# A GNN, attention and expert layer: the edge count, the turned tiles, the keys' copies, the stores and the norm's groups rearranged

## The chip, the core and the metric

The kernel runs on one core of one Trainium2 chip. It is written against the core's engines: TensorE (PE in the profile; the loads of its weights are listed apart as PEld), VectorE (DVE), ScalarE (ACT), GpSimd (POOL) and SyncE (SP), which only issues transfers. ScalarE and GpSimd also issue transfers from their own instruction streams; the profile lists these issues as ACTq, POOLq or POOL DMA_DIRECT2D. The metric is the time of one execution in microseconds (us), lower is better. All data are float32, apart from the 0/1 masks of the edge count, which are bfloat16.

## What is computed

N = 1250 rows of D = 768 features, and E = 21,250 edges (10,000 random pairs in both directions, and a loop at each node) sorted by their target. Cut to what matters:

```python
edge_index = jnp.stack([src, dst])
xn = _layernorm(x)
x = x + gnn(xn, edge_index) + mix(xn)
x = x + ffn(_layernorm(x))

def gnn(x, edge_index):          # two graph attention layers, then one product
    x_norm = layer_norm(x, norm_g, norm_b)
    out1 = gat_conv(x_norm, ..., W1, 4 heads of 192)
    out2 = gat_conv(out1, ..., W2, 2 heads of 96)
    return concatenate([x, out2]) @ Wu + bu

def mix(x):                      # linear attention, 12 heads of 64, then an MLP
    h = layer_norm(x, ln1_w, ln1_b)
    q, k, v = split(h @ qkv_w + qkv_b); q, k = elu(q) + 1, elu(k) + 1
    kv = einsum('hsd,hse->hde', k, v); z = 1 / einsum('hsd,hd->hs', q, k.sum(s))
    x = x + einsum('hde,hsd,hs->hse', kv, q, z) @ proj_w + proj_b
    h = layer_norm(x, ln2_w, ln2_b)
    return x + gelu(h @ fc1_w + fc1_b) @ fc2_w + fc2_b

def ffn(x):                      # 4 experts, the gates from the mean over all rows
    ...
```

gat_conv weighs each edge by a softmax over the edges of its target. The same pair can occur several times among the edges, and then counts as often.

## The kernel before

**Tiles and stages.** The rows are cut into NT = 10 tiles of TP = 125; the 768 features into KC = 6 parts of 128 for TensorE's contraction, and into two output halves of 384 (HALVES). Two large buffers, slot_a and slot_x, hold changing things: acc (L67) is ten tiles of raw x in slot_a, xn (L68) ten normalized tiles in slot_x, and fT [128, 6, 1250] the rows turned (features on partitions). The stages, in time order (us from the span's start):

1. to 32: the attention vectors are folded into W1 (turned_weights, folded); the result is fx.
2. 31 to 120: the loop over tiles at L488: normalized(t) (L404, one ScalarE instruction) writes xn; six transposes ps_t (L496) and two ScalarE copies (L499) turn the tile into fT; ps_u (L503) is the tile times Wu, 24 TensorE instructions, and VectorE adds it to acc (L508). So each tile's products begin with transposes and end before the next tile's transposes.
3. 120 to 213, the "g loop" at L527: norms(t + 1) (L467) brings the next tile through two more norms: a transpose of the row scales (ps_r, L472), a VectorE product into zT or in place into fT (L480), and six affines for each, alternating between VectorE (even k, L338) and ScalarE (odd k, L334). Then ps_g (L536) is zT times fx, 24 instructions; ScalarE copies it into gt (L541), VectorE copies the attention scores s (L542), and SyncE stores gt to g1_d in DRAM. zT and gt have two buffers each in the pool pk.
4. 213 to 297 keys, then values, queries (375 to 460), products of quarters: each pair of tiles needs seven products (a Strassen form) with the intermediate tiles c1, u2 and ex (keys_pair L614, values_pair L654, queries L698).
5. 457 to 541: the projection ps_p (L913), with a norm after it in groups of tiles, order2 (L900): moments on VectorE, then z on ScalarE (L936), six transposes (L943) and affines into fT.
6. 541 to 1357: the MLP (fc1 L127 and L81, fc2 L1016) mixed with the two graph attention layers; 1357 to the end: the experts.

**Edges.** The attention is computed on a dense matrix of edge counts, tabs[0] and tabs[1] in DRAM. Each edge has a key (target times N plus source, kcol: one column of 125 keys for each of 170 groups). edge_piece(i) (L282) handles 17 columns: kr (L275, 1 MB, the keys of these groups broadcast to all partitions) is compared with kcol (L292, eq), summed (L296, mult: how often the edge's key occurs in its group), multiplied by a lower triangle mask `before` (L297), summed again (L301, first), turned into first = 0 or 1 (L302), and then into a place (L304, L307): the key itself for the first occurrence, a row of trash otherwise. 17 indirect scatters from POOL (L309) add mult at place, alternately to the two tables. Pieces 0 to 5 are placed in the ps_u loop at tiles 1, 2, 4, 5, 7, 8 (`pieces`), pieces 6 to 9 in the g loop at odd tiles. The keys of pieces 0 to 3 are loaded from POOL's queue, each issued where piece i − 2 is (load_keys, L272); the later ones from SyncE's. The scatters to one table wait for each other's landing.

**What sets the order.** The program is written in one stream; the framework places the waits from the reads and writes of tiles and from the reuse of buffers, and may move instructions of one engine ahead of each other by its own priorities, except where the helpers `pin`, `vec`, `act`, `mat` (L71 to L83) keep the written order. So the built order is not the written one: among others, the first (k = 0) matmuls of some tiles' ps_g stand before the rest of an earlier tile's.

**Stores.** by_parts (L91) splits each store of a tile in two issues (112 and 13 partitions) and pins it. In the g loop raw x goes to raw_d (at t = 4 and 5, five tiles each, from ScalarE's queue) and xn to xn_d (at t = 6 to 9, two, two, two and four tiles, from ScalarE's queue too). Both are read back later: xn_d before the projection, raw_d in the graph stage. slot_x is then overwritten by the keys: y1 and y2 in keys_pair are kk, a view of slot_x.

**Places.** Keys' and values' c1, u2 and kex are tiles of the pool kvp, opened after pk is closed and so laid into the place of zT and gt; queries' copies qc1, qu2, qex lie in the pool qp, together with z2 (L934, one buffer) of the norm stage. The pool mk (opened at t == 8 in the g loop on the right side, where the edges' pool ep was before edges.close()) holds wsum, same, kvbd, ksum and later wq.

Of the kernel before, what the change touches and what calls it, by code (L numbers as in the profile page):

```python
# [8 lines left out]
F32 = mybir.dt.float32  # L9
# [17 lines left out]
PIECE = 17  # L27
# [5 lines left out]
def tile_gps_layer(ctx, tc, a, out):  # L33
# [212 lines left out]
    def columns():  # L246
# [12 lines left out]

    before = ep.tile([128, TP], BF16, name="before")  # L260
    nc.gpsimd.memset(before, 1.0)
    nc.gpsimd.affine_select(
        out=before, in_=before, compare_op=ALU.is_ge, fill=0.0, base=-1,
# [18 lines left out]
    def edge_piece(i):  # L282
# [13 lines left out]
        nc.vector.tensor_reduce(mult[:, c0 : c0 + PIECE], eq, AX.X, ALU.add)  # L296
        nc.vector.tensor_tensor(  # L297
            eq, eq, before[:TP].unsqueeze(1).to_broadcast([TP, PIECE, TP]), ALU.mult
        )
        first = ep.tile([TP, PIECE], F32, name="first", bufs=2)  # L300
        nc.vector.tensor_reduce(first, eq, AX.X, ALU.add)  # L301
        nc.vector.tensor_scalar(first, first, 0.0, None, op0=ALU.is_equal)  # L302
# [185 lines left out]
    for t in range(NT):  # L488
        tc_ = slice(t * TP, (t + 1) * TP)
        if t:  # L490
            normalized(t)
        for j in range(2):
            ps = bank4("ps_t")
            for i in range(3):
                k = 3 * j + i
                nc.tensor.transpose(  # L496
                    ps[:, i, :TP], xn[:, t, k * 128 : (k + 1) * 128], ident[:TP, :TP]
                )
            nc.scalar.copy(fT[:, 3 * j : 3 * j + 3, tc_], ps[:, :3, :TP])  # L499
        for c0, w in HALVES:  # L500
            ps = bank("ps_u")
            for k in range(KC):
                nc.tensor.matmul(  # L503
                    ps[:TP, :w], fT[:, k, tc_], wu[:, k, c0 : c0 + w],
                    start=k == 0, stop=k == KC - 1,
                )
            o = acc[:, t, c0 : c0 + w]
            nc.vector.tensor_tensor(o, ps[:TP, :w], o, ALU.add)  # L508
        for t0, n in SPLITS[1:]:
            if t == t0 - 2:  # L510
                for t1 in range(t0, t0 + n):
                    moments(acc[:, t1, :], mv[:, t1, :], vec)
                scales(t0, n)
        if t == 8:
            ahead = norms(0)
        if t in pieces:
            edge_piece(pieces[t])
# [9 lines left out]
    for t in range(NT):  # L527
# [21 lines left out]
        if t in (4, 5):  # L549
            for i in range(5 * t - 20, 5 * t - 15):  # L550
                by_parts(nc.scalar, raw_d[i], acc[:, i, :])
        if t > 5:
            for i in ((0, 5), (1, 6), (2, 7), (3, 8, 4, 9))[t - 6]:
                by_parts(nc.scalar, xn_d[i], xn[:, i, :])
# [16 lines left out]
        if t == 8:  # L571
            edges.close()
            mk = mix.enter_context(tc.tile_pool(name="mk", bufs=1, side="right"))
            wsum = mk.tile([128, 3, 3, 384], F32, name="wsum")
            wk7 = seven_weights(wk, wsum)
            by_tokens(nc.vector, xt, 0, TP)
# [9 lines left out]
    with tc.tile_pool(name="kvp", bufs=1) as kvp:  # L586
# [27 lines left out]
        def keys_pair(t):  # L614
# [4 lines left out]
            c1 = u3 = kvp.tile([TP, 384], F32, name="c1", bufs=2)  # L619
            u2 = kvp.tile([TP, 384], F32, name="u2", bufs=2)  # L620
# [3 lines left out]
            def put(o, p, q):  # L624

                nc.vector.tensor_tensor(o, p, q, ALU.add)
                ex = kvp.tile([TP, 384], F32, name="kex", bufs=2)
# [26 lines left out]
        def values_pair(t, vs):  # L654
# [4 lines left out]
            c1 = u3 = kvp.tile([TP, 384], F32, name="c1", bufs=2)  # L659
            u2 = kvp.tile([TP, 384], F32, name="u2", bufs=2)  # L660
# [37 lines left out]
        def queries(i, c):  # L698
# [5 lines left out]
            c1 = u3 = qp.tile([128, 375], F32, name="qc1", bufs=2)[:, :w]  # L704
            u2 = qp.tile([128, 375], F32, name="qu2", bufs=2)[:, :w]
# [4 lines left out]
            def put(o, p, k):  # L710
                ex = qp.tile([128, 375], F32, name="qex", bufs=2)[:, :w]
# [122 lines left out]
    with tc.tile_pool(name="qp", bufs=1) as qp:  # L834
# [65 lines left out]
        order2 = [(0, 1, 5, 6), (2, 3, 7), (4, 8, 9)]  # L900
# [4 lines left out]
        for part in order2:  # L905
# [27 lines left out]
            for t in part:  # L933
                z = qp.tile([TP, D], F32, name="z2", bufs=1)  # L934
# [865 lines left out]
```

## Time and profile before

| what | us |
|---|---|
| runs | 1912.76, 1917.06, 1915.63 (median 1915.63) |
| the profiled execution, its own time | 1917.79 |
| its span on the core | 1915.70 |
| TensorE's granted clock, mean over the span | 0.993 |
| busy: ScalarE / GpSimd | 802.8 / 502.7 |

The span is from the first to the last instruction that the profiler saw; the profiled execution's own time is 2.09 us longer. Busy times of the engines by stage, from the table of stretches (PE, VectorE and ScalarE, and PE's granted clock in it):

| stretch | length | PE | DVE | ACT | clock |
|---|---|---|---|---|---|
| 31 to 120, ps_u | 89.0 | 86.07 | 64.42 | 18.46 | 1.00 |
| 112 to 226, g loop to keys' start | 114.0 | 102.69 | 96.36 | 33.95 | 0.96 |
| 226 to 243, first keys | 17.0 | 15.86 | 9.50 | 6.07 | 0.85 |
| 243 to 541, keys to projection | 298.0 | 297.46 | 165.42 | 74.42 | 1.00 |
| 541 to 556, the last norm group | 15.0 | 10.71 | 9.12 | 8.92 | 0.89 |

Lines of the timeline begin with the start and the duration of an instruction, or of several alike joined together (x6), both in us; then engine, line, operation, output and inputs; and in brackets how long the engine had been idle before, and what ended it. Lines of the groups give busy time and the mean in ns of one instruction after the first bar, and the idle time just before them after the second.

### The profile page before, as it was taken

Reading aid. Unit: us, or ns where it says so; the run is one execution under the profiler, and the core shown is the slowest. Engines: PE = TensorE matmul, PEld = TensorE weight load, DVE = VectorE, ACT = ScalarE, POOL = GpSimd, SP = SyncE. Lnnn points to the kernel's source line nnn. Section 1 sums busy time; section 2 is a strip of 40 time slices with the busy share of each in tenths; the row PEclk is TensorE's granted clock in tenths of the full one; section 3 lists DMA queues with packets and bytes.
Section 4 is the critical chain, followed back from the end, with each engine's and each line's share of the span. In section 5 each row is a group of like instructions: output and inputs, shape, how many; then the busy total and the mean of one; then the engine's idle time right before and its main releaser. Section 6 shows DMA issues by size and latency. Waiting matters only on the chain.

```text
span 1915.7 us, 19523 instructions
## 1 busy us (share of the span) xinstructions
PE 1872.7 (98%) x6966; PEld 1244.2 (65%) x6966; DVE 1355.5 (71%) x2372; ACT 802.8 (42%) x1206; POOL 502.7 (26%) x341
## 2 busy tenths in 40 slices
PE   8999899999999999999999999999999999999998
PEld 7555456775556667787877655566766666666664
DVE  4889651379545986676766977865787777777778
ACT  3223231232321117777775166754473343533330
POOL 2167588777851110020210111100131000000000
PEclk9999999999999999999999999999999999999999
DMA  9957711423149742242432542301485201011023
GB/s 342 274 133 177 200 1 2 116 18 66 2 34 158 142 111 76 70 118 74 113 100 56 149 121 82 92 9 52 130 95 90 76 1 66 1 66 38 20 85 110
DMA packets 184284, 175.49 MB, mean 92 GB/s; under 512 B 110043, under 2 KB 153595, under 8 KB 182908
## 3 DMA queue, kind: packets, MB, share of 16 engines
q0 software_dynamic: 126640, 68.01, 20.7%
q1 hardware_dynamic: 54270, 98.48, 16.3%
q10 hardware_dynamic: 3278, 7.75, 1.3%
q8 instruction: 55, 0.90, 0.2%
q14 instruction: 41, 0.34, 0.1%
HBM read 137.80 MB, written 42.05 MB: 94 GB/s over the span
## 4 chain that ended last, share of the span: by engine, by line
PE 87%; DMA 5%; DVE 3%; issue 2%; ACT 1%; SPq 1%; POOL 0%; DVEq 0%; POOLq 0%; ACTq 0%
PE ps_f L1016 15%; PE ps_p L81 13%; PE ps_r L81 12%; PE ps_a L127 8%; PE ps_o L1194 7%; PE ps_p L913 4%; PE ps_c L127 4%; PE ps_g L536 3%; PE ps_f L1594 3%; PE ps_o L1233 2%; PE ps_va L127 2%; PE ps_qa L127 2%; PE ps_ka L127 2%; PE ps_d L127 2%; PE ps_u L1246 1%
## 5 line engine op out<-in xcount | busy, mean ns | idle before, releaser
L309 POOL DMA_INDIRECT tab<-mult,place_e x170 | 355.7, 2092 | 149.5 <-DMA tab<-mult,place_e 99.0
L1016 PE MATMUL ps_f<-w,v 128*125 128x384 f32 x960 | 337.5, 486 | 0.0
L1016 PEld LDWEIGHTS ps_f<-w,v 128*125 128x125 f32 x960 | 177.7, 188 | 106.0 <-issue 7.5
L1021 DVE TENSOR_TENSOR slot_a<-ps_f,slot_a 125x384 f32<-125x384 f32 x240 | 131.5, 552 | 66.5 <-PE ps_f L1016 62.6
L1149 DVE TENSOR_TENSOR wt<-ee 125x375 f32<-125x375 f32 (+1 forms) x180 | 105.8, 589 | 85.8 <-PE ps_o L1194 57.5
L1194 PEld LDWEIGHTS ps_o<-turns,wt 125*125 125x125 f32 x800 | 136.9, 188 | 29.7 <-DVE wt L1150 4.5
L1194 PE MATMUL ps_o<-turns,wt 125*125 125x193 f32 x800 | 151.6, 329 | 3.5 <-DVE wt L1150 3.5
L1144 ACT ACTIVATE ee<-bt,s 125x375 f32<-125x375 f32 (+1 forms) x180 | 114.8, 638 | 78.0 <-DVE wt L1149 69.5
L81 PE MATMUL ps_p<-fT,w 128*128 128x312 f32 (+1 forms) x432 | 125.5, 426 | 2.1 <-DMA w<-in_L_ffn_w_dram 1.5
L1150 DVE SCALAR_TENSOR_TENSOR wt<-wt,slot_x 125x375 f32<-125x375 f32 (+1 forms) x180 | 105.9, 589 | 4.4
L81 PEld LDWEIGHTS ps_p<-fT,w 128*128 128x128 f32 x432 | 81.5, 189 | 37.9 <-issue 1.7
L81 PE MATMUL ps_r<-w,slot_a 128*125 128x384 f32 x260 | 94.5, 486 | 0.0
L536 PE MATMUL ps_g<-fx,zT 128*125 128x388 f32 x240 | 83.6, 507 | 5.7 <-DVE zT L338 5.2
L127 PE MATMUL ps_a<-fT,w 128*128 128x250 f32 (+1 forms) x288 | 85.4, 426 | 0.7 <-DVE slot_a L918 0.7
L1556 DVE SCALAR_TENSOR_TENSOR slot_x<-ps_r,gate,slot_x 125x384 f32<-125x384 f32 x100 | 60.7, 615 | 33.3 <-PE ps_r L81 33.0
L81 PE MATMUL ps_p<-xt,ws 128*128 128x313 f32 (+1 forms) x288 | 83.6, 425 | 0.0
L503 PE MATMUL ps_u<-wu,fT 128*125 128x384 f32 x240 | 80.0, 490 | 2.4 <-ACT fT L499 2.4
L913 PE MATMUL ps_p<-wp,slot_x 128*125 128x384 f32 x240 | 79.5, 486 | 0.0
L1086 DVE SCALAR_TENSOR_TENSOR slot_x<-turns,s,slot_x 125x1250 f32<-125x1250 f32 x54 | 79.4, 1509 | 0.1
L1147 ACT ACTIVATE ee<-bt,s1l 125x375 f32<-125x375 f32 (+1 forms) x120 | 75.4, 628 | 0.1
L965 ACT ACTIVATE v<-v,par 128x250 f32<-128x250 f32 (+1 forms) x72 | 40.0, 556 | 78.1 <-DVE v L985 31.7
L81 PE MATMUL ps_r<-w2s,ht 128*125 128x384 f32 x200 | 72.7, 486 | 0.0
(403 smaller groups left out, 3432.1 us busy)
## 6 DMA issues: line engine op xcount, KB each, us to landing
turns<-g_d POOLq DMA_DIRECT2D x12, 942.4 KB
w<-in_L_mix_fc_w_dram SPq DMA_DIRECT2D x12, 768.0 KB
w<-in_L_mix_fc_w_dram SPq DMA_DIRECT2D x24, 384.0 KB
slot_x<-tab POOLq DMA_DIRECT2D x14, 610.4 KB
w<-in_L_ffn_w_dram SPq DMA_DIRECT2D x11, 768.0 KB
w<-in_L_ffn_w_dram SPq DMA_DIRECT2D x5, 1536.0 KB
slot_x<-tab POOLq DMA_DIRECT2D x40, 183.1 KB
kr<-key_d SPq DMA_DIRECT2D x6, 1062.5 KB
```

The lines of the kernel that those rows point to most:

```text
L81: return lambda *args, **kw: pin(getattr(self.engine, name)(*args, **kw))
L127: engine.matmul(ps, wt[:, k, :], x[:, k, :], start=k == 0 and not more, stop=k == n - 1, skip_group_check=more,)
L309: nc.gpsimd.indirect_dma_start(out=tabs[c % 2][:, :], out_offset=bass.IndirectOffsetOnAxis(ap=place[:, c : c + 1], axis=0), in_=mult[:, c ...
L503: nc.tensor.matmul(ps[:TP, :w], fT[:, k, tc_], wu[:, k, c0 : c0 + w], start=k == 0, stop=k == KC - 1,)
L536: nc.tensor.matmul(ps[:TP, :388], zT[:, k, :], fx[:, k, h2 * 388 : (h2 + 1) * 388], start=k == 0, stop=k == KC - 1,)
L913: nc.tensor.matmul(ps[:TP, :w], qT[:, k, t * TP : (t + 1) * TP], pm[:, k, c0 : c0 + w], start=k == 0, stop=k == KC - 1,)
L1016: nc.tensor.matmul(ps, v_of[c][:, f, h, at : at + TP], lasts[g, j][:, f, :], start=f == 0, stop=f == 1,)
L1021: nc.vector.tensor_tensor(o, ps, o, ALU.add)
L1144: nc.scalar.activation(e[:, 0, :w], bt[:TP, 0, :w], AF.Exp, bias=s[:, 0, h, c : c + 1])
L1149: nc.vector.tensor_tensor(wt[:, :w], e[:, 0, :w], e[:, 1, :w], ALU.max)
L1150: nc.vector.scalar_tensor_tensor(wt[:, :w], wt[:, :w], 1.0, adj, op0=ALU.min, op1=ALU.mult)
L1194: nc.tensor.matmul(sums[i // 2][:TP, (i % 2) * 193 : (i % 2 + 1) * 193], wt[:, i * TP : (i + 1) * TP], gh[:, c, :], start=c == 0 and i % 2 ...
```

## The change

It has five parts.

1. `before` holds 256 on and 1 off the strict lower triangle, in place of 1 and 0. One reduction after the multiplication gives mult, and first is mult < 256. The reduction of eq before the multiplication falls away. For an edge that is the first of its key in its group the sum is the old count; for another it is larger, and such edges go to the trash rows.
2. The transposes and copies of a tile become a function, turned_x; turned_x(t + 1) stands between the two halves of tile t's ps_u, and normalized(t + 1) before them.
3. c1, u2 and ex of keys, values and queries come from one helper, between, with two buffers each of [128, 384] in the pool mk.
4. raw_d is stored at t = 2 and 3 of the g loop (five tiles each), xn_d at t = 4 to 8 (two tiles each).
5. The last group (4, 8, 9) of the norm becomes (4, 8) and (9,), and z2 has two buffers.

```diff
--- before.py
+++ after.py
@@ -257,10 +257,11 @@
     before = ep.tile([128, TP], BF16, name="before")
-    nc.gpsimd.memset(before, 1.0)
+    nc.gpsimd.memset(before, 256.0)
     nc.gpsimd.affine_select(
-        out=before, in_=before, compare_op=ALU.is_ge, fill=0.0, base=-1,
+        out=before, in_=before, compare_op=ALU.is_ge, fill=1.0, base=-1,
         pattern=[[-1, TP]], channel_multiplier=1,
     )
     mult = const.tile([TP, EC], F32, name="mult")
@@ -293,13 +294,12 @@
             eq, kr[:TP], kcol[:, c0 : c0 + PIECE].unsqueeze(2).to_broadcast([TP, PIECE, TP]),
             ALU.is_equal,
         ))
-        nc.vector.tensor_reduce(mult[:, c0 : c0 + PIECE], eq, AX.X, ALU.add)
         nc.vector.tensor_tensor(
             eq, eq, before[:TP].unsqueeze(1).to_broadcast([TP, PIECE, TP]), ALU.mult
         )
+        nc.vector.tensor_reduce(mult[:, c0 : c0 + PIECE], eq, AX.X, ALU.add)
         first = ep.tile([TP, PIECE], F32, name="first", bufs=2)
-        nc.vector.tensor_reduce(first, eq, AX.X, ALU.add)
-        nc.vector.tensor_scalar(first, first, 0.0, None, op0=ALU.is_equal)
+        nc.vector.tensor_scalar(first, mult[:, c0 : c0 + PIECE], 256.0, None, op0=ALU.is_lt)
         at = ep.tile([TP, PIECE], F32, name="at_e", bufs=2)
         nc.vector.scalar_tensor_tensor(
             at, kcol[:, c0 : c0 + PIECE], trash, first, op0=ALU.subtract, op1=ALU.mult
@@ -485,10 +485,8 @@
         return zT
 
     pieces = {1: 0, 2: 1, 4: 2, 5: 3, 7: 4, 8: 5}
-    for t in range(NT):
-        tc_ = slice(t * TP, (t + 1) * TP)
-        if t:
-            normalized(t)
+
+    def turned_x(t):
         for j in range(2):
             ps = bank4("ps_t")
             for i in range(3):
@@ -496,8 +494,18 @@
                 nc.tensor.transpose(
                     ps[:, i, :TP], xn[:, t, k * 128 : (k + 1) * 128], ident[:TP, :TP]
                 )
-            nc.scalar.copy(fT[:, 3 * j : 3 * j + 3, tc_], ps[:, :3, :TP])
+            nc.scalar.copy(
+                fT[:, 3 * j : 3 * j + 3, t * TP : (t + 1) * TP], ps[:, :3, :TP]
+            )
+
+    turned_x(0)
+    for t in range(NT):
+        tc_ = slice(t * TP, (t + 1) * TP)
+        if t + 1 < NT:
+            normalized(t + 1)
         for c0, w in HALVES:
+            if c0 and t + 1 < NT:
+                turned_x(t + 1)
             ps = bank("ps_u")
             for k in range(KC):
                 nc.tensor.matmul(
@@ -546,11 +554,11 @@
         by_parts(nc.sync, g1_d[:, t * TP : (t + 1) * TP, :].rearrange("h p f -> p h f"), gt)
         if t % 2 and t < 9:
             edge_piece(6 + t // 2)
-        if t in (4, 5):
-            for i in range(5 * t - 20, 5 * t - 15):
+        if t in (2, 3):
+            for i in range(5 * t - 10, 5 * t - 5):
                 by_parts(nc.scalar, raw_d[i], acc[:, i, :])
-        if t > 5:
-            for i in ((0, 5), (1, 6), (2, 7), (3, 8, 4, 9))[t - 6]:
+        if 4 <= t < 9:
+            for i in (t - 4, t + 1):
                 by_parts(nc.scalar, xn_d[i], xn[:, i, :])
         if t == 2:
             vec.tensor_tensor(arow[:, 0, :], arow[:, 0, :], arow[:, 1, :], ALU.add)
@@ -571,6 +579,10 @@
         if t == 8:
             edges.close()
             mk = mix.enter_context(tc.tile_pool(name="mk", bufs=1, side="right"))
+
+            def between(name):
+                return mk.tile([128, 384], F32, name=name, bufs=2)
+
             wsum = mk.tile([128, 3, 3, 384], F32, name="wsum")
             wk7 = seven_weights(wk, wsum)
             by_tokens(nc.vector, xt, 0, TP)
@@ -616,15 +628,15 @@
             w11, w12, s3, w22, s1, s2, s4 = wk7
             x11, x21, x22, t3, t1, t2, t4 = tokens_side(t * TP, TP)
             pa, pd, pc = (bank(n)[:TP, :384] for n in ("ps_ka", "ps_kd", "ps_kc"))
-            c1 = u3 = kvp.tile([TP, 384], F32, name="c1", bufs=2)
-            u2 = kvp.tile([TP, 384], F32, name="u2", bufs=2)
+            c1 = u3 = between("c1")[:TP]
+            u2 = between("u2")[:TP]
             b0, b1 = kb[:, :384], kb[:, 384:]
             y1, y2 = kk[:, t, :], kk[:, t + 5, :]
 
             def put(o, p, q):
 
                 nc.vector.tensor_tensor(o, p, q, ALU.add)
-                ex = kvp.tile([TP, 384], F32, name="kex", bufs=2)
+                ex = between("ex")[:TP]
                 nc.scalar.activation(ex, o, AF.Exp)
                 nc.scalar.activation(o, o, AF.Relu)
                 nc.vector.scalar_tensor_tensor(o, ex, 1.0, o, op0=ALU.min, op1=ALU.add)
@@ -656,8 +668,8 @@
             w11, w12 = wv[:, 0:3, 0:384], wv[:, 3:6, 0:384]
             x11, x21, x22, t3, t1, t2, t4 = tokens_side(t * TP, TP)
             pa, pd, pc = (bank(n)[:TP, :384] for n in ("ps_va", "ps_vd", "ps_vc"))
-            c1 = u3 = kvp.tile([TP, 384], F32, name="c1", bufs=2)
-            u2 = kvp.tile([TP, 384], F32, name="u2", bufs=2)
+            c1 = u3 = between("c1")[:TP]
+            u2 = between("u2")[:TP]
             y1, y2 = vs
 
             def blocks(p):
@@ -701,14 +713,14 @@
             c0, w = MIX[c]
             x11, x21, x22, t3, t1, t2, t4 = tokens_side(c0, w)
             pa, pd, pc = (bank(n)[:, :w] for n in ("ps_qa", "ps_qd", "ps_qc"))
-            c1 = u3 = qp.tile([128, 375], F32, name="qc1", bufs=2)[:, :w]
-            u2 = qp.tile([128, 375], F32, name="qu2", bufs=2)[:, :w]
+            c1 = u3 = between("c1")[:, :w]
+            u2 = between("u2")[:, :w]
             va1, va2, vb1, vb2 = (
                 qT[:, k, h + c0 : h + c0 + w] for k in (i, i + 3) for h in (0, HALF)
             )
 
             def put(o, p, k):
-                ex = qp.tile([128, 375], F32, name="qex", bufs=2)[:, :w]
+                ex = between("ex")[:, :w]
                 nc.scalar.activation(ex, p, AF.Exp, bias=pvec("q_b", k))
                 nc.scalar.activation(o, p, AF.Relu, bias=pvec("q_b", k))
                 nc.vector.scalar_tensor_tensor(o, ex, 1.0, o, op0=ALU.min, op1=ALU.add)
@@ -897,7 +909,7 @@
 
         mv2 = const.tile([TP, NT, 2], F32, name="mv2")
         r2 = const.tile([TP, NT, 2], F32, name="r2")
-        order2 = [(0, 1, 5, 6), (2, 3, 7), (4, 8, 9)]
+        order2 = [(0, 1, 5, 6), (2, 3, 7), (4, 8), (9,)]
         for part in order2:
             for t in part:
                 by_parts(nc.sync, xn[:, t, :], xn_d[t])
@@ -931,7 +943,7 @@
                 nb, mv2[:, ts, 0], -1.0, r, op0=ALU.mult, op1=ALU.mult
             )
             for t in part:
-                z = qp.tile([TP, D], F32, name="z2", bufs=1)
+                z = qp.tile([TP, D], F32, name="z2", bufs=2)
                 i = where[t]
                 nc.scalar.activation(
                     z, xn[:, t, :], AF.Identity, bias=r2[:, i, 1:2], scale=r2[:, i, 0:1]
```

## The prediction

> **What bounds the kernel now.** I read the busy table first, then TensorE's waits, then the timeline around each wait, then the groups of VectorE.
>
> ```profile
> PE 1872.7 (98%) x6966; PEld 1244.2 (65%) x6966; DVE 1355.5 (71%) x2372; ACT 802.8 (42%) x1206; POOL 502.7 (26%) x341
> ...
> PE ps_g L536 <- DVE zT L338: 5.2, 2, 2.7
> PE ps_ka L127 <- DVE c L633: 4.7, 1, 4.7
> ...
> PE ps_t L943 <- ACT z L936: 2.9, 3, 1.8
> ...
> PE ps_u L503 <- ACT fT L499: 2.4, 9, 0.4
> ```
>
> TensorE sets the end: 1872.7 of 1915.7 us, so at most 43.0 us are idle. The waits (total, times, longest) of the lines that the change touches are small. But idle time has a second cost: after some waits the same matmuls run at half rate.
>
> ```profile
> 131.42 9.78 PE L536 MATMUL ps_g<-fx,zT 128*125 128x388 f32 x24 [2.68 <-DVE zT L338]
> ...
> 191.03 22.39 PE L536 MATMUL ps_g<-fx,zT 128*125 128x388 f32 x68 [2.56 <-DVE zT L338]
> ...
> 226.49 4.20 PE L127 MATMUL ps_ka<-wsum,slot_a 128*125 128x384 f32 x6 [4.68 <-DVE c L633]
> ...
> 232.01 2.10 PE L127 MATMUL ps_ka<-wk,fT 128*125 128x384 f32 x6
> ```
>
> Columns: start, duration, and in brackets the idle time before and what ended it. Six matmuls take 4.20 and, shortly after, 2.10; 24 of L536 take 9.78 where the tile before takes 7.98. So a wait costs its idle time plus 1.4 to 2.2 us. VectorE bounds 97 to 131 us and shares the g loop (102.69 TensorE, 96.36 VectorE busy from 112 to 226).
>
> **(a) Edge count and turned tiles.**
>
> ```profile
> L301 DVE TENSOR_REDUCE first<-eq 125x17 f32<-125x2125 bf16 x10 | 23.6, 2362 | 0.2
> ...
> 88.02 1.40 POOL L275 DMA_DIRECT2D kr<-key_d  x1
> 94.79 2.02 POOL L309 DMA_INDIRECT tab<-mult,place_e  x1 [5.38 <-DMA tab<-mult,place_e]
> ...
> 97.46 2.37 DVE L292 TENSOR_TENSOR eq<-kr,kcol 125x2125 bf16<-125x2125 f32 x1 [5.67 <-DMA kr<-key_d]
> ```
>
> The change removes L301: ten reductions of 2.36 us, 23.6 of VectorE. The comparison with 256 keeps the form of L302. Most of the 23.6 lies beside TensorE's work. It counts where VectorE is last, from the comparison of piece 3 at 97.46 to ps_g of tile 1 at 131.42: 33.96 us, of which 6.9 are three of the reductions (the last ends after its cover begins). Without them 27.1, or 28.4 if one run of three ScalarE affines (1.25 us) loses its cover; I take 28.4. Against it stands the load of piece 3's keys on POOL's queue. In the built order it stands behind four scatters instead of three, and these wait for one another's landing (idle 11.15 and 5.38 before those at 86.79 and 94.79). The first scatter comes a reduction earlier (2.4); one more landing costs 5.4 to some 13 (two scatters start 13.2 apart). I take a load at about 90 instead of 88.02: 2 later (range 1 to 10; further landings are a rival below). Then ps_g of tile 1 starts at 97.46 + 2 + 28.4 = 127.9, a gain of 3.5. TensorE could allow it: each of nine tiles' transposes loses its wait on the copy (1.05 us from first transpose to first product at L496; 0.73 where the norm stage already has work between, 496.51 to 497.24), 9 × 0.32 + 0.56 = 3.4, and ps_g of tile 1 then has 2.7 idle of its own to give. Gain **3.5**, between −4.5 (load 10 later) and 7.8 (TensorE's 3.4 + 2.7, and 1.7 at half rate).
>
> **(b) Stores in the g loop.** Their issues sit on ScalarE's queue, in front of its affines of zT and its copies of gt:
>
> ```profile
> 177.15 8.16 ACTq L94 DMA_DIRECT2D raw_d<-slot_a  x7
> 185.41 1.25 ACT L334 ACTIVATE zT<-zT,par 128x125 f32<-128x125 f32 x3 [8.33 <-DMA raw_d<-slot_a]
> ```
>
> Now the ten issues of tile 5 (9.87 us with the three before these; those of tile 4 took 7.48) hold up zT of tile 7, and ps_g waits 1.18 + 0.50 + 2.56 = 4.24, plus 1.7 at half rate: 5.9 lost. The change moves both batches to tiles 2 and 3 and gives tiles 4 to 8 only four xn_d issues each (2.72 and 2.91 in the rows of tiles 6 and 7, no wait behind them). Let X be the end of tile 2's product. In the built order the k = 0 matmuls of tiles 4 and 5 (1.3 us each) come before the rest of tile 4 (6.5), and those of tile 6 before the rest of tile 5. So TensorE has work to X + 8.0 + 2 × 1.3 + 0.5 (transposes) = 11.2. Queued behind the batch at tile 2 are ScalarE's affines for tile 4: with some 7 us of issues, 9.4 to 10.7, so no wait. Behind the batch at tile 3 (9.9 from 12.7, after gt's copies) are those for tile 5, done at 22.9; and the next edge piece starts only after tile 3's copies, 12.4 + (2.36 + 1.27 + 2.36 + 0.7) = 19.1 on VectorE, with zT of tile 6 (0.93 + 0.34) behind it, 20.6. TensorE is free at 11.2 + 6.5 = 17.7: 3.0 idle, then 0.7 until 22.9, and 1.7 at half rate: 5.4 lost. Moved, not removed: gain 0.5, and the lighter VectorE (one reduction in these tiles) makes it **1.0**. Bounds from the issue row (303/414/1450 ns): at 1450 each, the nine issues take 6.0 longer, 5.5 of it idle, and the ten 4.6 longer on top of 3.7, with 1.7 at half rate 15.5 lost (−9.6); with no wait, +5.9.
>
> The Trainium skill ("DMA: Bandwidth & Descriptors", section "Issuing engines are not separate DMA queues") says that transfers of all issuing engines run on the same 16 engines and interleave. It speaks against the new place: tiles 2 and 3 also carry key loads and scatters. The trace agrees in part: three issues took 2.34 us, seven took 8.16.
>
> **(c) Keys' first product.** Before, c1, u2 and ex lay in the place of gt and zT, so the first c1 waited for gt's last store:
>
> ```profile
> 225.88 1.02 DVE L633 TENSOR_TENSOR c<-ps_ka,kvb 125x384 f32<-125x384 f32 x2 [7.89 <-DMA g_d<-gt]
> ```
>
> Keys begin at 213.26; by 242.37, 60 matmuls are done, 60 × 0.3225 = 19.35 of 29.1 us: 9.8 lost (4.68 idle and 2.2 at half rate, the rest in shorter gaps). In the new pool the tiles lie where the edges' tiles were, last read by VectorE itself. What is late next: y1's write waits for xn_d stores (its tile is their source), which are issued two tiles earlier, the last four at tile 8 instead of eight at 213.47; and the exponential's table load (1.28). I keep 1.3 lost: gain **8.5** (6.9 if only the first wait and its half rate go, 9.8 at most, 1 to 2 if the stores hold y1 as long).
>
> **(d) Norm groups.**
>
> ```profile
> 547.45 0.89 PE L943 MATMUL ps_t<-ident,z 125*128 125x125 f32 x6 [0.54 <-ACT z L936]
> 550.14 0.89 PE L943 MATMUL ps_t<-ident,z 125*128 125x125 f32 x6 [1.81 <-ACT z L936]
> ...
> 552.18 2.87 PE L127 MATMUL ps_a<-xt,ws 128*128 128x250 f32 x6 [1.15 <-ACT c L982]
> ```
>
> With (4, 8, 9) last, three tiles' norms and transposes stand after the last product: 0.65 + 0.14 + 0.54 + 1.81 + 1.15 = 4.3 idle, and 1.4 + 0.2 at half rate (2.87 against 1.43): 5.9. With (9,) alone last, tiles 4 and 8 are normed and turned beside tile 9's products, two z2 buffers let the second begin; what stays is 0.65 + 0.14 + 0.1 and one wait like that at 518.81 (0.54): gain **4.5** (3 if the half rate stays, 5.9 at most).
>
> Weighed against the rows: the Trainium skill ("TensorE: Matmul & The Clock Gate", "Why this matters for your kernels") has the clock fall only after idle gaps over some 3 us. The trace disagrees: half rate follows 2.68, 2.56 and 1.81 + 1.15. By that rule only the 4.68 would give its half rate back, and the sum would be about 15.9 instead of 17.5.
>
> **(e) The rest: 0.** Later the built order is the same on VectorE, TensorE and ScalarE. The GNN stage first needs the table at 607.5; POOL's scatters, back to back, end at 558.4 and the first chunk lands near 574.5: 33 us of cover. They hardly move, so a lead beyond 33 would be lost; 17.5 is not.
>
> **Sum:** 3.5 + 1.0 + 8.5 + 4.5 = 17.5. The profiled execution took 1917.79 with span 1915.70 (2.09 around it), 2.2 above the median 1915.63 of runs that spread over 4.3; the gain is taken from the median: 1915.63 − 17.5 = **1898.1**.
>
> **Rivals.**
> - Stores block ScalarE at tiles 2 and 3 at 1450 ns each: (b) is −9.6 instead of 1, time 1909. For: seven issues took 8.16. Against: ten of tile 4 took 7.48 and nothing waited.
> - Keys' wait changes its name: xn_d stores hold y1; (c) is 1.5, time 1905. For: kk's tile is the stores' source, and the first exponential follows xn_d issues. Against: four issues instead of eight, earlier.
> - All stalls vanish: 7.8 + 5.9 + 9.8 + 5.9 = 29.4, time 1886. For: each has a named cause that the change addresses. Against: VectorE keeps 96.36 − 5 × 2.36 = 84.6 us of work in the g loop.
> - Slower: the piece-3 keys, behind a fourth scatter, come late by L instead of 2. The gain is 17.5 + 2 − L, lost beyond L = 19.5. Two further landings of 12.9 give 25.8: 1922. For: landings before took 5 to 13 with loads running, and the stores come earlier. Against: only one scatter more stands ahead.
> - That it does nothing is excluded: in the built order the reductions are gone and the transposes and stores have moved.
>
> **Chances.** Forecast 0.52 (own range 1889 to 1905), stores 0.14, keys 0.08, all vanish 0.13, slower 0.13. What a measurement can tell from no change is 0.2%, 3.8 us. Faster: 0.52 + 0.08 + 0.13 + 0.12 of the stores case = 0.85; slower 0.10 and same 0.05 (0.03 of the slower case, 0.02 of the stores case). The range runs from 1884 (1886 less half the runs' spread) to 1911 (1909 plus it), and leaves out little but the slower case.
>
> **What would show it.** One reduction of 10 × 2.36 instead of two. L503 without its wait on fT. The comparison of piece 3 at about 99.5; past 107 (a) is wrong. Keys' c1 no longer released by a store, its L127 rows at 2.10; if y1 (L626) waits for xn_d, the second rival. ps_g's waits in tiles 4 to 7 near 3.7 in all; over 10, the first. L943 waits under 1 and no 2.87 row. L1082's first instruction not waiting for a load. A gain outside these four places would make the working wrong even with the time right.

## The result, and the profile after

The changed kernel took 1901.84 us (median of five runs, 1896.16 to 1903.77) against 1915.63 before (five runs, 1912.76 to 1919.16): a ratio of 0.9924, with a 95% interval from 0.9902 to 0.9945. The forecast was 1898, in a range from 1884 to 1911: the gain is 13.8 us of the 17.5 that were forecast. The profiled execution took 1899.71, with a span of 1897.80.

The line numbers after are 1 to 12 higher than before: L301 is gone and L296 has become L300, L503 is L511, L536 is L544, L943 is L955, L1054 is L1066, L1067 is L1079, L1082 is L1094. First the busy table of the changed kernel, from its page, then its VectorE groups, then TensorE's waits:

```profile
PE 1869.2 (98%) x6966; PEld 1245.8 (66%) x6966; DVE 1333.8 (70%) x2365; ACT 803.5 (42%) x1207; POOL 506.8 (27%) x341
```

```profile
L300 DVE TENSOR_REDUCE mult<-eq 125x17 f32<-125x2125 bf16 x10 | 23.6, 2357 | 0.1
```

```profile
PE ps_g L544 <- DVE zT L338: 3.0, 2, 1.8
...
PE ps_g L544 <- DVE at_e L304: 2.3, 1, 2.3
...
PE ps_t L955 <- ACT z L948: 1.2, 2, 0.6
...
PE ps_u L511 <- ACT fT L497: 0.4, 1, 0.4
```

VectorE lost 21.7 us of work, TensorE only 3.5 (in part fewer products at half rate). Most of what the kernel gained is in the waits: L511's went from nine to one, and the wait of L127 for c is no longer in the list.

Most of what follows reads one number off each profile: the **lead**, how many us earlier than in the kernel before TensorE starts the same product. Where the lead changes, time was won or lost. For the changed kernel:

| TensorE reaches | lead, us | step of the forecast |
|---|---|---|
| first ps_u | −0.16 | |
| ps_g of tile 0 | 2.74 | |
| ps_g of tile 1 | 3.49 | (a) 3.5: grew by 3.65 |
| ps_g of tiles 2 and 3 | 5.19 | the half rate behind the old wait: 1.70 |
| first key product | 7.24 | (b) 1.0: grew by 2.05 |
| projection | 15.38 | (c) 8.5: grew by 8.14 |
| fc1 product, at 560.24 before | 20.54 | (d) 4.5: grew by 5.16 |
| around 700 us | 20.53 | (e) 0 |
| the end | 17.90 | (e) 0: lost 2.63 |

The places that the prediction named, in TensorE's timeline after:

```profile
127.93 8.09 PE L544 MATMUL ps_g<-fx,zT 128*125 128x388 f32 x24 [1.83 <-DVE zT L338]
...
164.35 2.62 PE L544 MATMUL ps_g<-fx,zT 128*125 128x388 f32 x4 [2.27 <-DVE at_e L304]
166.76 0.62 PE L472 MATMUL ps_r<-ident,rst 125*128 125x125 f32 x2
...
209.89 2.10 PE L127 MATMUL ps_ka<-wsum,slot_a 128*125 128x384 f32 x6
...
531.12 0.86 PE L955 MATMUL ps_t<-ident,z 125*128 125x125 f32 x6
...
533.13 1.53 PE L127 MATMUL ps_a<-xt,ws 128*128 128x250 f32 x6
```

ps_g of tile 1 starts at 127.93 (forecast 127.9). The wait in the g loop has moved to tile 5 (forecast 3.0 + 0.7 and half rate; found 2.27 + 0.41, and four matmuls in 2.62 where they take 1.47). The third key product has no wait before it and runs at full rate; only one set of transposes is left behind the last projection product.

But the five runs spread over 7.6 us (the kernel before: 6.4), and the median gained 13.8 where this profile gained 17.9. The experiments had to find where the rest goes.

### The profile page after: what moved, and what is told of

It is laid out like the page before. It is cut to its first block, busy times and chain, and to the rows that moved or that the text cites. A ratio compares the mean times of both kernels' runs of the same rounds, so it can differ in the third digit from the quotient of the medians.

```text
span 1897.8 us, 19510 instructions
## 1 busy us (share of the span) xinstructions
PE 1869.2 (98%) x6966; PEld 1245.8 (66%) x6966; DVE 1333.8 (70%) x2365; ACT 803.5 (42%) x1207; POOL 506.8 (27%) x341
## 3 DMA queue, kind: packets, MB, share of 16 engines
q0 software_dynamic: 126640, 68.01, 20.7%
## 4 chain that ended last, share of the span: by engine, by line
PE 87%; DMA 4%; issue 4%; DVE 3%; ACT 1%; POOL 0%; ACTq 0%; DVEq 0%; POOLq 0%; SPq 0%
PE ps_f L1028 15%; PE ps_p L81 13%; PE ps_r L81 12%; PE ps_a L127 8%; PE ps_o L1206 7%; PE ps_p L925 4%; PE ps_c L127 4%; PE ps_f L1606 3%; PE ps_o L1245 2%; PE ps_va L127 2%; PE ps_ka L127 2%; PE ps_g L544 2%; PE ps_qa L127 2%; PE ps_d L127 2%; PE ps_u L1258 1%
## 5 line engine op out<-in xcount | busy, mean ns | idle before, releaser
L1033 DVE TENSOR_TENSOR slot_a<-ps_f,slot_a 125x384 f32<-125x384 f32 x240 | 131.5, 553 | 67.4 <-PE ps_f L1028 63.7
L544 PE MATMUL ps_g<-fx,zT 128*125 128x388 f32 x240 | 81.7, 496 | 5.7 <-DVE zT L338 3.0
L127 PE MATMUL ps_a<-fT,w 128*128 128x250 f32 (+1 forms) x288 | 85.4, 426 | 0.6 <-DVE slot_a L930 0.6
L511 PE MATMUL ps_u<-wu,fT 128*125 128x384 f32 x240 | 79.9, 487 | 0.4 <-ACT fT L497 0.4
```

The lines of the kernel that those rows point to most:

```text
L127: engine.matmul(ps, wt[:, k, :], x[:, k, :], start=k == 0 and not more, stop=k == n - 1, skip_group_check=more,)
L511: nc.tensor.matmul(ps[:TP, :w], fT[:, k, tc_], wu[:, k, c0 : c0 + w], start=k == 0, stop=k == KC - 1,)
L544: nc.tensor.matmul(ps[:TP, :388], zT[:, k, :], fx[:, k, h2 * 388 : (h2 + 1) * 388], start=k == 0, stop=k == KC - 1,)
L1033: nc.vector.tensor_tensor(o, ps, o, ALU.add)
```

## The experiments

Each kernel is the changed one with one edit (x10 and x11 with two and three, x12 with none), and computes the same. x1 to x8 ran once each: 1906.10, 1901.34, 1903.25, 1899.44, 1902.92, 1906.49, 1909.57 and 1895.67 us in that order, where one run of the kernel before took 1914.65 beside the first four and 1917.84 beside the others. Single times tell little where runs of the changed kernel spread over 7.6 us, so these eight are read by their leads, each from one profiled execution:

| kernel | tile 1 | tile 3 | keys | projection | fc1 | at 700 | end |
|---|---|---|---|---|---|---|---|
| changed | 3.49 | 5.19 | 7.24 | 15.38 | 20.54 | 20.53 | 17.90 |
| x1_two_sums | −1.63 | −1.62 | −0.81 | 7.32 | 12.49 | 12.48 | 11.32 |
| x2_turned_before | −2.96 | −2.96 | 1.65 | 9.79 | 15.23 | 15.22 | 16.46 |
| x3_copies_in_place | 1.56 | 3.26 | 7.86 | 12.73 | 17.91 | 17.88 | 14.36 |
| x4_stores_before | 0.55 | 2.24 | 6.11 | 14.25 | 19.42 | 18.62 | 18.26 |
| x5_three_groups | −1.11 | 0.58 | 5.20 | 13.32 | 16.01 | 15.37 | 14.86 |
| x6_one_z2 | 2.04 | 3.73 | 6.58 | 14.72 | 20.22 | 9.56 | 11.16 |
| x7_keys_on_sync | 6.44 | 8.13 | 11.64 | 19.77 | 25.53 | 9.76 | 8.08 |
| x8_raw_on_sync | 1.65 | 3.34 | 10.19 | 18.32 | 24.10 | 21.62 | 21.81 |
| x12_changed_again | −0.12 | 1.57 | 6.18 | 14.32 | 19.50 | 14.85 | 16.02 |
| x9_tail | 0.62 | 2.31 | 6.91 | 15.04 | 20.47 | 20.46 | 20.55 |
| x10_tail_raw | 0.61 | 2.34 | 9.19 | 17.32 | 23.20 | 23.20 | 19.84 |
| x11_all | 6.99 | 8.78 | 15.63 | 23.76 | 29.03 | 18.97 | 19.16 |

**Two sums again.**

```diff
-    nc.gpsimd.memset(before, 256.0)
+    nc.gpsimd.memset(before, 1.0)
...
+        nc.vector.tensor_reduce(mult[:, c0 : c0 + PIECE], eq, AX.X, ALU.add)
         nc.vector.tensor_tensor(
             eq, eq, before[:TP].unsqueeze(1).to_broadcast([TP, PIECE, TP]), ALU.mult
         )
-        nc.vector.tensor_reduce(mult[:, c0 : c0 + PIECE], eq, AX.X, ALU.add)
+        nc.vector.tensor_reduce(first, eq, AX.X, ALU.add)
+        nc.vector.tensor_scalar(first, first, 0.0, None, op0=ALU.is_equal)
```

> The changed kernel with the edge count's two reductions back (mask 1 and 0, sum before and after the multiplication), all else as changed. Lead means how much earlier than in the kernel before TensorE reaches a point; in the changed kernel it is 2.74 us at the first ps_g, 3.49 at ps_g of tile 1, 5.19 at tile 2, 7.24 at the first key product, 17.7 at the end. Theory (VectorE sets ps_g of tile 1, the reductions are the gain there): the lead at tile 1 falls by the three reductions, 6.9, less the 1.8 that TensorE waits there now, to -2 to 0, the half rate after that wait comes back, and the g loop loses 2 to 5 more. Rival (the turned tiles give the lead, VectorE has slack): the lead at tile 1 falls by less than 1.5.

VectorE's and TensorE's timelines of this kernel:

```profile
99.08 2.45 DVE L293 TENSOR_TENSOR eq<-kr,kcol 125x2125 bf16<-125x2125 f32 x1 [7.59 <-DMA kr<-key_d]
```

```profile
133.05 9.78 PE L545 MATMUL ps_g<-fx,zT 128*125 128x388 f32 x24 [2.69 <-DVE zT L339]
```

From the comparison of piece 3 to ps_g of tile 1 it takes 133.05 − 99.08 = 33.97, as before the change (33.96), against 127.93 − 101.00 = 26.93 in the changed kernel: three reductions are worth 7.0 here, and the half rate (9.78) is back. The theory holds: the lead at tile 1 is −1.63, and from there to the keys it grows by 0.82 instead of 3.75. The lead at tile 1 fell by 5.1, not 6.9, since the comparison came 1.9 earlier: with two sums the key load stands behind three scatters again.

**Transposes between the tiles again**, with normalized(t) and the six transposes back ahead of both halves of tile t.

> The changed kernel with each tile's transposes back between the products of two tiles. Theory: the lead at the first ps_g falls from 2.74 to about 0 (nine waits of 0.32), but ps_g of tile 1 is set by VectorE, so there the lead falls by under 1.5 (3.49 to 2 or more), and the end loses as little. Rival (TensorE's own order sets the stage): the 2.9 are lost at tile 1 and at the end too.

The stage from the first ps_u to its last product took 90.1 us, against 84.2 in the changed kernel and 88.5 before. 1.6 of it are half rate in the first tile, where 24 products take 9.62 and in the next tiles 8.01; the other 88.5 are what the stage took before. So in this stage the turned tiles save TensorE 4.3, where the prediction worked out 3.4. But the lead at tile 1 also fell, by 6.45, far over the bound, and what set it was piece 3's load: the comparison came at 107.22, 6.2 later (here the load stands behind five scatters), and ps_g of tile 1 followed 27.16 behind it. So the run shows who sets tile 1, and not what the turned tiles are worth there apart from the load; that stays open. The lead at the end, 16.46, lies between the changed kernel's two profiles (17.90 and 16.02): a loss there can't be told.

**The copies in their old place** (c1, u2 and ex from kvp and qp, as before the change).

> The changed kernel with c1, u2 and ex of keys, values and queries back in their own pools, over the place of zT and gt. Theory: the first c1 waits for gt's last store again, 4 to 5 us idle and 2 at half rate; between the first key product and the end of the keys the lead grows by 1 to 3 instead of 8.1. Rival (the earlier xn stores are what freed the keys): it still grows by 6 or more.

TensorE's timeline, and VectorE's:

```profile
215.95 2.20 PE L127 MATMUL ps_ka<-wsum,slot_a 128*125 128x384 f32 x6 [2.00 <-DVE c L642]
```

```profile
215.34 1.02 DVE L642 TENSOR_TENSOR c<-ps_ka,kvb 125x384 f32<-125x384 f32 x2 [8.36 <-DMA g_d<-gt]
```

The wait for gt's store is back, so the place is its cause. But it costs 2.00 and no half rate, and the lead still grows by 4.87 across the keys, between the two expectations. So without the new place the rest of the change still brings 4.9 of the 8.1. The rows say where: gt's last store was issued at 213.97 before and at 206.10 here, and VectorE's c came 11.9 and 9.2 behind it. That is 2.7 less of waiting, and the half rate behind it, 2.2, is gone. Why the store lands sooner was only argued: eight xn issues left together with it before, and none does now. That was not tried alone.

**The stores in their old place** (raw_d at tiles 4 and 5, xn_d at 6 to 9).

> The changed kernel with the raw stores back at tiles 4 and 5 and the xn stores at tiles 6 to 9. Theory: the g loop loses 1 to 4 of its lead (two batches block ScalarE there as in the kernel before, 3 to 6 lost instead of 4.3), and the keys lose at most 2 of their 8.1, to the xn stores. Rival (the xn stores at tile 9 hold the keys as much as the place of the copies did): the keys lose 4 or more.

The keys gain 8.14, all of it: with the copies elsewhere, the stores don't hold the keys. The loss in the g loop that the theory had did not come: from tile 3 to the keys the lead grows by 3.87, against 2.05 in the changed kernel's profile and 4.61 in its second one (4.6 also in x2, x3, x5 and x9, 2.85 in x6). Moving the raw stores from tiles 4 and 5 to 2 and 3 was worth under 1, if anything. "Moved, not removed" holds.

**One last group** ((4, 8, 9), z2 with two buffers), and **one z2** (the changed groups, one buffer).

> The changed kernel with the norm's last groups (4, 8) and (9,) as one group (4, 8, 9) again, z2 with two buffers. In the changed kernel the lead grows by 5.16 us from the projection's start to the first fc2 product (15.38 to 20.54). Theory (the last group's norms stand behind the last product): it grows by 0 to 1.5 only. Rival (the second z2 buffer is what took the waits away): it grows by 3 or more.

> The changed kernel with z2 in one buffer. Theory (the groups do it; the second buffer only lets tile 8's z begin while tile 4's is turned, beside a product): the growth of 5.16 us from the projection to the first fc2 product falls by 0 to 1. Rival (the buffer): by 2 or more.

With one last group the lead grows by 2.69 from the projection to fc1, instead of 5.16: between the two expectations. 1.6 of the 2.69 are the half rate, which did not come here (the first fc1 product behind the transposes takes 1.53, before 2.87); the idle time fell only from 4.3 to 3.4. So the second buffer helps a last group of three by about 1, and the rest hung on the clock (last section). With the split groups it isn't needed: one buffer, 5.50. The same run showed what nobody had expected. TensorE, then VectorE, at the start of the graph stage with one z2:

```profile
605.16 2.92 PE L1028 MATMUL ps_f<-w,v 128*125 128x384 f32 x4 [8.79 <-DVE slot_a L1033]
```

```profile
599.87 1.06 DVE L1094 TENSOR_SCALAR turns<-slot_x 125x1250 f32<-125x1250 f32 x1 [12.46 <-DMA slot_x<-tab]
```

fc2's products wait 8.79 us for VectorE to free their banks (L1033), because VectorE's queue stands at L1094, which waits 12.46 us for the first chunk of the edge table. The lead falls from 20.22 to 9.56. The edit of z2 touches nothing of the table; but the last scatter into the table came at 567.27 here, against 559.03 in the changed kernel's profile.

**Piece 3's keys from SyncE.**

```diff
-            load_keys(i + 2, nc.gpsimd)
+            load_keys(i + 2, nc.sync if i else nc.gpsimd)
```

> The changed kernel with one edit: the load of piece 3's keys is issued from SyncE instead of from behind four scatters on GpSimd's queue. In four runs with one reduction per piece ps_g of tile 1 came 26.9 to 27.2 us after the comparison of piece 3, which waited 11.6 to 14.1 us for that load. Theory (this load sets ps_g of tile 1): the comparison starts near 90 instead of 101, ps_g of tile 0 and 1 no longer wait (1.2 and 1.8 in the changed kernel), and the lead at ps_g of tile 2 rises from 5.2 to 8 to 9. Rival (the landings are slow because all transfers share the engines; the load lands as late from any queue): the comparison stays at 98 or later and the lead under 7.

```profile
98.05 2.38 DVE L293 TENSOR_TENSOR eq<-kr,kcol 125x2125 bf16<-125x2125 f32 x1 [8.76 <-DMA kr<-key_d]
```

ps_g of tiles 0 and 1 no longer wait, and the lead at tile 2 is 8.13, as the theory had it. But the load, issued some 16 us earlier, brought the comparison only to 98.05, as the rival had it: probably because it now shares the engines with piece 4's load, issued right behind it, which no run tried apart. And all of it was lost at the graph stage:

```profile
605.17 2.92 PE L1028 MATMUL ps_f<-w,v 128*125 128x384 f32 x4 [14.12 <-DVE slot_a L1033]
```

14.12 us of waiting, and the lead falls from 25.53 to 9.76.

**Raw stores from SyncE.**

```diff
-                by_parts(nc.scalar, raw_d[i], acc[:, i, :])
+                by_parts(nc.sync, raw_d[i], acc[:, i, :])
```

> The changed kernel with one edit: raw_d is stored from SyncE's queue instead of ScalarE's, at the same tiles 2 and 3. Between ps_g of tile 3 and the first key product the changed kernel gained 2.05 us on the kernel before, the one with the stores in their old place 3.87. Theory (the issues block ScalarE's affines and copies, and VectorE's edge piece behind them): the waits of 2.27 and 0.41 and the half rate behind them go, and the gain is 5 to 6.5. Rival (VectorE is what is late there, or the transfers themselves are in the way of the keys' loads): the gain stays under 3.

The lead grows by 6.85 from tile 3 to the keys, a little over what the theory had, and ps_g runs without a wait behind tile 1. What blocked there can be read in the changed kernel's ScalarE row, 10.59 us behind raw stores:

```profile
167.25 0.49 ACT L334 ACTIVATE zT<-zT,par 128x125 f32<-128x125 f32 x1 [10.59 <-DMA raw_d<-slot_a]
```

The issues on ScalarE's queue were the cause, not the transfers: with the same bytes on SyncE's queue no wait is left. This holds in x10 and x11 too, 6.85 each. Their worth is 2.2 us against the 4.6 of most kernels with the issues on ScalarE, and 4.8 only against the changed kernel's first profile.

**The changed kernel again, and the table's end.** In the built order the first scatters go to one table only (three before, four in the changed kernel), so the last ones all go to the other (four and five) and wait for each other: the last three scatters before, and the last four now, stand idle some 2 us each for a landing. x9 sends two of the last columns to the first table:

```diff
-                out=tabs[c % 2][:, :],
+                out=tabs[c % 2 if c < EC - 4 else 0][:, :],
```

x10 adds the raw stores on SyncE, x11 also piece 3's keys (with EC − 6). All four were timed on one chip, beside the kernel before:

> The changed kernel itself, again, beside the next three. Theory (the lead of about 20 us at the graph stage has used up the cover of the edge tables, whose last scatter falls between 555 and 570 us from run to run; where it falls late, fc2 waits): the runs spread over 6 us or more, and the profile shows either no wait or one of 5 to 14 us of the fc2 products for VectorE near 590 us. Rival (the spread comes from the half clock alone): no such wait, a spread of 2 to 4 us.

> The changed kernel with two of the last columns' scatters sent to the other table (both tables are added up later), so that the last scatters alternate; before, the last five or six went to one table and waited 1.9 us each for one another. Theory: the last scatter is issued some 8 us earlier (545 to 558), VectorE's wait for the first chunk (2.3 in the changed kernel, 12 to 18 in two runs) goes, and the median is 0 to 5 us under the changed kernel's in the same call, with a smaller spread. Rival (the table is not what varies): median within 1 us of it.

> As x9_tail, with the raw stores issued from SyncE. Theory: the g loop's 2.3 + 0.4 us of waits go (as in x8_raw_on_sync, where the lead grew by 6.85 from tile 3 to the first key product instead of 2.05), and the median is 3 to 6 us below x9_tail's. Rival (the lead is lost again at the graph stage): less than 1.5 us below.

> As x10_tail_raw, with piece 3's keys loaded from SyncE (and three columns sent to the other table, since the scatters then start with six to one table). Theory: ps_g of tiles 0 and 1 no longer wait (x7_keys_on_sync: lead 6.44 at tile 1), 2 to 5 us below x10_tail_raw if the table comes in time. Rival (the table's cover is used up again): no lower than x10_tail_raw, with fc2 waiting near 590 us.

| kernel | median (lowest to highest) | ratio to before, 95% interval |
|---|---|---|
| before, beside them | 1918.17 (1916.05 to 1919.53) | |
| x12_changed_again | 1906.03 (1901.72 to 1912.11) | 0.9946, 0.9932 to 0.9960 |
| x9_tail | 1897.89 (1897.19 to 1899.37) | 0.9898, 0.9883 to 0.9913 |
| x10_tail_raw | 1894.44 (1892.72 to 1897.64) | 0.9874, 0.9859 to 0.9889 |
| x11_all | 1904.04 (1898.31 to 1905.45) | 0.9927, 0.9913 to 0.9940 |

The last scatter, in GpSimd's timeline of the changed kernel again, and of x9:

```profile
564.29 1.99 POOL L309 DMA_INDIRECT tab<-mult,place_e  x1 [2.02 <-DMA tab<-mult,place_e]
568.23 4.64 POOL L1066 DMA_DIRECT2D tab<-tab  x3 [1.96 <-DMA tab<-mult,place_e]
580.30 0.58 POOL L1079 DMA_DIRECT2D slot_x<-tab  x1 [7.42 <-PE ps_f L1028]
```

```profile
555.79 1.99 POOL L309 DMA_INDIRECT tab<-mult,place_e  x1 [0.30 <-issue]
560.70 4.65 POOL L1066 DMA_DIRECT2D tab<-tab  x3 [2.92 <-DMA tab<-mult,place_e]
572.17 0.57 POOL L1079 DMA_DIRECT2D slot_x<-tab  x1 [6.82 <-ACT u L1004]
```

VectorE's first instruction on the table, in the same two:

```profile
594.73 0.81 DVE L1094 TENSOR_SCALAR turns<-slot_x 125x1250 f32<-125x1250 f32 x1 [6.59 <-DMA slot_x<-tab]
```

```profile
587.54 1.11 DVE L1094 TENSOR_SCALAR turns<-slot_x 125x1250 f32<-125x1250 f32 x1 [0.38 <-DMA slot_x<-tab]
```

Two changed columns, 8.1 us less (1906.03 to 1897.89, more than the 0 to 5 expected), and a spread of 2.2 us instead of 10.4. In x9 VectorE's wait at L1094 is 0.38; in the changed kernel's second profile it was 6.59, TensorE's behind it 2.69 (less than the 5 expected) with half rate after it, and the lead fell from 19.50 to 14.85. That profile is of the fastest of the five runs (1901.72); the slower four were not profiled. So the theory holds: the lead of 20 us had used up the table's cover, the time that passes before VectorE wants the table. x10 has the lowest median of this case, 3.45 us under x9, as expected (their intervals overlap by a little); x11 has the largest lead of all at fc1 (29.03), and VectorE waits 10.80 us for the table: no gain, as its rival had it.

The last column of the table of leads doesn't follow from the one before it alone: from 700 us to the end, where all the kernels are alike, the changed kernel lost 2.6, x10 lost 3.4, and x9 nothing. Half rate has a part in that (last section).

## Why the prediction was right, and where it was not

**(a) Edges and turned tiles.** Right in the sum by two errors that met. The chain from the comparison to ps_g of tile 1 was 26.9, the lower bound, where I took 28.4; the load came 3.5 late where I took 2. The mechanism, the key load behind a fourth scatter, is the better part of the reading: in nine executions of this stage as changed the comparison started between 101.00 and 105.60, and ps_g of tile 1 came 26.9 to 27.7 behind it. But its size was off for most of them: the first profile was the luckiest. The lead at tile 3, 5.19 there, has a median of 2.3 over the nine (0.58 to 5.19). The load's delay, taken as 2, has a median of 5.6. What tile 1 loses comes back in part: at the first key product the six profiles with (a) and (b) as changed show leads of 5.20 to 7.86. The turned tiles saved TensorE 4.3 in their stage, not 3.4. The slower rival (L over 19.5) did not occur; the worst was 8.1.

**(b) Stores in the g loop.** Right in the mechanism: the wait moved to the tiles named, with 2.27 and 0.41 where 3.0 and 0.7 were worked out, behind the row named. The size was again that of the first profile: in x2, x3, x5, x9 and x12 the whole wait is 1.50 with no half rate behind it, and the lead grows by 4.6 instead of 1.0. The first rival (1450 ns an issue) did not occur. The rule of the Trainium skill ("DMA: Bandwidth & Descriptors", "Issuing engines are not separate DMA queues") that issuing from another engine saves only the issuing engine's own time fits x8: with the issues off ScalarE no wait is left between tile 3 and the keys.

**(c) Keys.** Right in the cause, and in the size by luck: 8.14 against 8.5, and 8.1 in every run with the new place. The prediction counted 60 products done by 242.37 and so 9.8 lost. In the trace 60 are done by 240.75 and 66 by 242.69, which is 8.14 lost; and the 1.3 that was to stay lost did not stay. All of the 8.14 came back. That the xn stores would be what is late next was wrong. That 4.9 of it would come without the new place was not foreseen.

**(d) Norm groups.** Right; 5.16 instead of 4.5. Half of it (2.69) also came with the old groups and a second z2, most of that because the half rate fell away (x5).

**(e) "The rest: 0" is the step that failed.** I had the last scatter hardly move, the first chunk land at 574.5, 16 us behind it, and so 33 us of cover. Both were wrong. In the kernel before, GpSimd and VectorE:

```profile
555.33 3.08 POOL L309 DMA_INDIRECT tab<-mult,place_e  x1 [2.18 <-DMA tab<-mult,place_e]
...
571.32 0.57 POOL L1067 DMA_DIRECT2D slot_x<-tab  x1 [6.14 <-DVE slot_a L1021]
```

```profile
607.55 0.80 DVE L1082 TENSOR_SCALAR turns<-slot_x 125x1250 f32<-125x1250 f32 x1
```

No row there tells when the chunk landed; 574.5, some 3 us behind its issue, was assumed. The change moved a scatter from the alternating part to the one-table part at both ends, and the last one came at 559.0 to 567.3 (569.7 in x7) in the changed kernels, against 555.3 before (556.0 in x1, where three scatters stand ahead again). Why it spreads over 8 us where the scatters' order is the same is not shown. And the chunk was there not 3 us after its issue but 13 to 18: in the changed kernel's profile, GpSimd and VectorE,

```profile
559.03 1.99 POOL L309 DMA_INDIRECT tab<-mult,place_e  x1 [2.08 <-DMA tab<-mult,place_e]
...
573.60 0.58 POOL L1079 DMA_DIRECT2D slot_x<-tab  x1 [5.89 <-DVE slot_a L1033]
```

```profile
589.42 0.81 DVE L1094 TENSOR_SCALAR turns<-slot_x 125x1250 f32<-125x1250 f32 x1 [2.33 <-DMA slot_x<-tab]
```

the chunk is there 30.4 us after the last scatter (28.7 to 32.7 in the runs where VectorE waited for it). That L1082 (L1094 here) would not wait for a load was one of the prediction's own signs, and it failed. Counted so, the chunk was there at about 555.3 + 30.4 = 585.7 before the change, for an instruction at 607.55: 22 us of cover, not 33. x1, with its last scatter where it was before, has the landing in its trace: 585.6, 14.7 behind the issue. The waits come out of this sum. VectorE would be ready at 607.55 less the lead, and the chunk is later by just its wait: 588.05 and 594.73 in x12 (wait 6.59), 587.33 and 599.87 in x6 (12.46), 582.02 and 600.05 in x7 (17.94).

The forecast lead of 17.5 fitted under it; the lead that came, 20.5, reached its edge, and a late scatter took 5 us (x12) and 11 us (x6) back. This is the likely reason why the median gained 13.8 where (a) to (d) in the profile make 20.7 (1.7 of it the half rate behind tile 1's wait, which the sum did not have). The slower runs themselves were not profiled; but x9, where only the table's end differs, gains 20.3 in the median (1918.17 to 1897.89).

The row at 191.03 was also misread: I showed it among waits with half rate behind them, but its 68 matmuls took 22.39, 0.33 each, the full rate. The half rate counted there stands earlier, in the row at 179.34 (22 matmuls in 9.13), so the 5.9 of (b) holds.

## What to carry to other kernels

A saving early in a kernel is worth no more than the cover of the next transfer chain that doesn't get faster with it: follow that chain to the instruction that consumes its data, count landing times and not issues, and look at it again after the change. Where executions of one kernel spread more than those of another, look for such a race; here two columns out of 170 were worth as much as the largest part of the change. Here it paid to issue stores from the queue of an engine that computes nothing, and to alternate the targets to the very last scatter.

## What the hardware showed that was not expected

**The half rate is decided on a grid.** In the trace of the kernel before, the stretches at half clock begin at 131.97, 179.76, 224.13, 551.81 and 732.72 us: 14, 13, 96 and 53 times 3.413 us apart. Each lasts one such window or a few. Two idle times of nearly the same length, 2.68 (ended at 131.42) and 2.56 (ended at 191.03), in windows of that grid of the kernel before (busy us of PE, PEld, VectorE, ScalarE and GpSimd, each with its count, then PE's clock):

```profile
128.56:131.97 3.41, 0.73 (x4) 0.41 (x3) 3.41 (x7) 1.62 (x4) 0.00 (x0) 1.00 0.99 369
131.97:135.39 3.42, 3.42 (x7) 1.75 (x6) 3.40 (x11) 2.10 (x6) 0.70 (x1) 0.50 1.08 364
...
186.59:190.00 3.41, 1.88 (x6) 0.75 (x4) 1.49 (x2) 2.06 (x6) 2.37 (x2) 1.00 0.44 80
190.00:193.41 3.41, 2.38 (x8) 1.44 (x9) 3.41 (x6) 1.26 (x3) 2.34 (x1) 1.00 0.91 232
```

The first lies in one window (0.73 of 3.41 us busy), and the next runs at 0.50; the second is cut in two, and nothing happens. Over all runs, from 31 us on, every window with 2.05 us or more idle was followed by half rate; of the windows at full clock with 0.3 to 1.94 us idle, one was (1.68 us, the window before 179.76 of the kernel before). The Trainium skill ("TensorE: Matmul & The Clock Gate", "What's actually happening") has the same window of 3413 ns, free-running, and the grid agrees with it; the rule from its last part that I had weighed, gaps over some 3 us, is not what decides here. So here a wait of 2 to 3 us costs some 1.7 us more or nothing, by where it falls. Idle time is not all: at the entry to the experts, where TensorE runs transposes and products with 1 to 6 columns and is idle for only 0.26 us of a window, half rate followed in all thirteen profiles after the change, and in the one before it did not. Both go into the last column of the table of leads: from 700 us to the experts the changed kernel and x10 have four windows at half clock, x9 three and the kernel before one. The other part is a wait for VectorE near 1100 us (L1245): 1.10 in the changed kernel, 1.51 in x10, 0.94 before, and none in x9.
